# Two message-passing layers on one core: records of four numbers in the first sort, and edge groups in six steps

## The chip, the cores and the metric

The kernel runs on one NeuronCore of a Trainium2 chip. The metric is the time of one execution on the device in microseconds; lower is better. The engines are PE (TensorE: matmuls; PEld are its weight loads), DVE (VectorE), ACT (ScalarE), POOL (GpSimd, which also issues the indirect DMAs, that is gathers and scatters of rows) and SP (SyncE, which here only issues DMAs). Each takes its own instructions in order and waits on semaphores for the others.

## The reference

There are 3125 nodes with 256 features each, and 53125 edges, each with a source, a destination, a type (200 of them) and a weight. `src` comes in any order, `dst` is sorted. Four parts follow one another, each `x = x + part(layernorm(x))`:

```python
# 1: attention over edges, 4 heads of 64
feats = einsum('nd,hdo->hno', x, Ws) + bs
score = a_s[:, src] + a_d[:, dst] + aw_e * elem + ab
w = exp(-relu(score / 20))
out = segment_sum(w * feats[:, dst], src) / segment_sum(w, src)
# 2: 16 experts, the best two per node (silu-gated, hidden 512)
# 3: relations
score = h[src] @ w_src + h[dst] @ w_dst + rel_emb[etype] @ w_rel
alpha = exp(leaky_relu(score)); alpha = alpha / alpha
agg = segment_sum((h[src] + rel_emb[etype]) @ weight_neighbor * alpha, dst)
node = relu(agg) + where(in_degree > 0, h @ loop, h @ evolve_loop)
# 4: the better half of the nodes by a router goes through a 256-1024-256 gelu network
```

## The kernel before

Nodes are held in 25 blocks of 128. A layer over edges needs the edges sorted by the block that they add to.

**Sort of layer 0** (`sort_edges` with `roomy`). The edges lie 416 to a partition. From each edge's three values the kernel makes small whole numbers that float16 holds exactly (`dig`, V of them): the other node, the row in its block plus 1, and the 32 bits of the weight in three pieces of 11, 11 and 10 bits: V is 5. Places are counted with matmuls and scans. Then 13 blocks of columns are moved (`move`): for every eight columns DVE makes one-hot places (L577, L584) and products with the records (L593, one operation for two columns, 40 x V x 2 elements), and PE sums them into PSUM (L598). ACT copies a block's 40 x V numbers out (L606) and POOL scatters them in five indirect DMAs into a table in DRAM (L609). With all 65 scattered, `load` reads the table back (L629), turns it with PE and unpacks it on DVE (L650 to L661, `join_bits`), and writes a wide copy of the rows (`wide`) for later broadcasts. Layer 3's edges are taken in order, without this sort, in pieces that fill the steps of the first edge layer (`fill`).

**Edge layers** (`edge_stages`, `pipelined`). Every block has 18 tiles of 128 edges, the last 8, handled in groups of up to six: 74 groups and 440 tiles in each of the two edge layers. A group goes through three stages, one a step: in step s, group s is gathered, group s-1 becomes messages, group s-2 is added.

- `gather`: six indirect DMAs on POOL fetch the rows (L907) into one of 5 (first layer) or 4 (second) buffers `rows`; DVE makes a one-hot of each edge's row `oh` (L915) and, from the wide copy, transposed ones `hot` (L924).
- `message`: PE picks the near node's numbers with `hot` (L933) into PSUM, DVE sums them (L940), and `messages` makes the weights and scales: in the first layer ACT's exponential (L1097, L1098) and a product of the rows on DVE (L1099); in the second ACT scales `oh` into `ohw` (L1645), and DVE writes a one-hot of the edge type beside the rows (L1639). In a block's second group of the second layer, `loops` (called `early`) transposes the block's features and multiplies them by both loop weights (L200, L202, L1654) into `ps_hold`.
- `add`: PE multiplies `oh` by `rows` into the block's sum (L953, two instructions per tile). After a block's last group DVE reads the sum (L961) and `finish` follows at once. In the first layer it divides and updates x (L1110 to L1113), and at the ends of blocks 5, 10, 15, 20, 23 and 25 the gate's `done` normalizes, transposes and multiplies by the gate's weights (L190, L200, L202, L1196, L1200). In the second layer it turns the type counts (L1666, L1669), multiplies them by the relations (L1672), and DVE reads this and the loop products (L1679 to L1685).

The iota numbers that L915 and L1639 compare with stand in PSUM (`ps_hold`), as do the exponentials that L1099 multiplies by.

**Order.** Tiles, semaphores and the order of instructions on each engine come from a planner that takes the program's order as priority and may move an instruction ahead where its inputs are expected early; `keep_in_program_order` marks an instruction that keeps its place. A tile that is allocated in a full pool waits until the old tile's last reader is done, and the engine that first writes it waits with it.

**After the edges.** `router` prepares the last part, among others by loading its weights w1 and w2 (1 MB each) in a pool that is opened ahead of the second edge layer. `depths` picks the nodes and runs the network (L2016, L2028).

Of the kernel before, what the change touches and what calls it, by code (L numbers as in the profile page):

```python
# [12 lines left out]
I32 = mybir.dt.int32  # L13
AF = mybir.ActivationFunctionType
# [8 lines left out]
class _Kernel:  # L23
# [10 lines left out]


# [261 lines left out]
    def sort_edges(self, pool, rp, name, seg, other, value, bits, tab, help, roomy, into=()):  # L297
# [23 lines left out]
        def load_in():  # L321
# [21 lines left out]
            nc.vector.tensor_scalar(dig[:, 1, :], part, 1.0, None, op0=OP.add)  # L343
            nc.vector.tensor_scalar(dig[:, 0, :], oth_i, -float(self.half), None, op0=OP.add)
            if bits:
                for i, (sh, m) in enumerate(((0, 2047), (11, 2047), (22, 1023))):
                    v = tmp(I32)
                    nc.vector.tensor_scalar(
                        v, vi, sh, m, op0=OP.logical_shift_right, op1=OP.bitwise_and
                    )  # L350
                    nc.scalar.copy(dig[:, 2 + i, :], v)
            else:
                nc.scalar.copy(dig[:, 2, :], vi)
# [264 lines left out]
        def load():  # L618
# [4 lines left out]
            with tc.tile_pool(name=f"{name}_back", bufs=1) as bp:  # L623
# [29 lines left out]
                nc.vector.tensor_scalar(kept(st["row"]), turned(1), -1.0, None, op0=OP.add)  # L653
                for i, w in enumerate(wide):
                    wb = bp.tile([P, nb, P], BF16, name=f"{name}_wb{i}")
                    nc.vector.tensor_copy(wb[:m], tk[:m, :, :, 1 + i])
                    nc.sync.dma_start(w.rearrange("(i k) p -> k i p", k=m), wb[:m])
                if bits:
                    d = [bp.tile([P, MT], I32, name=f"{name}_d{v}") for v in range(3)]
                    for v in range(3):  # L660
                        nc.vector.tensor_copy(kept(d[v]), turned(2 + v))  # L661
                    self.join_bits(st["val"].bitcast(I32), d)
                else:
                    nc.vector.tensor_copy(kept(st["val"]), turned(2))
# [122 lines left out]
    def join_bits(self, out, d):  # L787
        nc = self.nc
        nc.vector.scalar_tensor_tensor(
            d[0], d[1], 11, d[0], op0=OP.logical_shift_left, op1=OP.bitwise_or  # L790
        )
        nc.vector.scalar_tensor_tensor(
            out, d[2], 22, d[0], op0=OP.logical_shift_left, op1=OP.bitwise_or
        )

# [11 lines left out]
    def edges_beyond(self, name, st, table, width, near, W, message, sums):  # L807
# [10 lines left out]
        with tc.If(more > 0):  # L818
            with tc.tile_pool(name=f"{name}_far", bufs=1) as pool:
# [6 lines left out]
                with tc.For_i(0, more) as k:  # L826
# [7 lines left out]
                    nc.vector.tensor_scalar(row, rec[:, 1:2], -1.0, None, op0=OP.add)  # L834
                    if V == 5:
                        d = tl("d", [3], I32)
                        nc.vector.tensor_copy(d, rec[:, 2:5])
                        self.join_bits(val.bitcast(I32), [d[:, i : i + 1] for i in range(3)])
                    else:
# [126 lines left out]
    def pipelined(self, stages, fill=()):  # L966
# [4 lines left out]
        for step in range(len(groups) + len(stages) - 1):  # L971
            if step > 2:
                next(fill, None)
# [1184 lines left out]
```

## Time and profile before

| | |
|---|---|
| median of 6 runs | 2305.77 us (2295.27 to 2313.69) |
| profiled execution | 2309.9 us, span 2308.2 us |
| sort of layer 0 | 0 to 281 us |
| first edge layer | 281 to 988 us |
| experts, and features for the second layer | 988 to 1428 us |
| second edge layer | 1428 to 2168 us |
| choice of nodes and the last network | 2168 to 2308 us |
| busy: PE, DVE, ACT, POOL | 1510.4, 1167.3, 425.5, 1128.8 us |
| mean granted PE clock | 0.799 |

The stages are read from the first and last gathers and from the names of the tiles. A row of the profile names the line, the engine, the operation, the tile written and the tiles read, how often, the busy time and the mean duration of one in ns, and behind the second bar the idle time of the engine just before such instructions with what ended it. "issue" is a wait that the profile can't tie to anything, "remote" a semaphore that was raised at a time where no recorded instruction raises it.

### The profile page before, as it was taken

How to read it: one execution, taken by the hardware profiler on the slowest of the kernel's cores; microseconds unless marked ns; L12 is line 12 of the kernel's file. 1: busy time of each engine (PE TensorE's matmuls, PEld its weight loads, DVE VectorE, ACT ScalarE, POOL GpSimd, SP SyncE). 2: the span in 40 equal slices, each digit the busy share in tenths (PEclk: the TensorE clock that was granted, in tenths of full speed). 3: DMA queues.
4: the chain of work that ended last, by engine and by line, in shares of the span. 5: the costliest groups of instructions: out<-in, count | busy, mean ns of one | idle time of the engine just before them, and what ended most of it. 6: DMA issues, size and time to landing. Idle time of an engine off the chain costs nothing. (4 is left out here: it accounts for less than half of the span.)

```text
span 2308.2 us, 22343 instructions
## 1 busy us (share of the span) xinstructions
PE 1510.4 (65%) x6602; PEld 940.8 (41%) x6602; DVE 1167.3 (51%) x3010; ACT 425.5 (18%) x1148; POOL 1128.8 (49%) x1133
## 2 busy tenths in 40 slices
PE   3688244353533544549999975577777777777588
PEld 1266133342432433426666643233333333333256
DVE  8999435453444643553322234354545555554641
ACT  1311000000101000102122224122222222222421
POOL 1078666656565665413333312455555555565151
PEclk7599667677666776659999988788888888888789
DMA  3050244443444443249999965544444444443230
GB/s 97 25 162 28 67 120 118 129 112 106 127 119 112 114 127 105 73 127 348 302 317 314 316 205 180 151 132 132 132 132 132 132 132 120 132 134 97 74 120 21
DMA packets 250714, 324.52 MB, mean 141 GB/s; under 512 B 38128, under 2 KB 185008, under 8 KB 250582
## 3 DMA queue, kind: packets, MB, share of 16 engines
q1 hardware_dynamic: 192214, 179.00, 25.0%
q0 software_dynamic: 51760, 137.35, 21.1%
q10 hardware_dynamic: 6608, 6.62, 0.8%
q8 instruction: 57, 0.93, 0.2%
q14 instruction: 75, 0.61, 0.1%
HBM read 286.26 MB, written 36.61 MB: 140 GB/s over the span
## 5 line engine op out<-in xcount | busy, mean ns | idle before, releaser
L907 POOL DMA_INDIRECT rows<-table,s_idx x880 | 839.0, 953 | 567.5 <-issue 294.5
L953 PE MATMUL ps_sums<-rows,oh 128*128 128x260 f32 x880 | 271.6, 474 | 246.1 <-issue 244.8
L953 PE MATMUL ps_sums<-rows,ohw 128*128 128x457 f32 x880 | 395.9, 597 | 12.2 <-issue 11.9
L953 PEld LDWEIGHTS ps_sums<-rows,oh 128*128 128x128 f32 x880 | 206.2, 241 | 298.7 <-issue 256.5
L953 PEld LDWEIGHTS ps_sums<-rows,ohw 128*128 128x128 f32 x880 | 177.7, 210 | 185.5 <-issue 171.9
L1387 PE MATMUL ps_h<-w,x_t 128*128 128x512 f32 x448 | 204.6, 599 | 0.0
L915 DVE TENSOR_TENSOR oh<-ps_hold,s_row 128x768 f32<-128x768 f32 (+1 forms) x148 | 139.6, 943 | 124.2 <-remote 74.5
L924 DVE TENSOR_SCALAR hot<-wide,pcols 128x768 bf16<-128x768 bf16 (+1 forms) x296 | 174.4, 596 | 26.5 <-remote 12.5
L1409 POOL DMA_INDIRECT ytab<-y,back x56 | 55.2, 985 | 203.0 <-DVE y L1408 194.2
L1645 ACT ACTIVATE ohw<-oh,s 128x128 f32<-128x128 f32 x440 | 136.8, 392 | 66.5 <-DVE s L1598 26.0
L1654 PE MATMUL ps_hold<-lw,x_t 128*128 128x512 f32 x100 | 78.9, 933 | 106.8 <-DVE oh L915 62.5
L1639 DVE TENSOR_TENSOR rows<-ps_hold,s_val 128x1200 f32<-128x1200 f32 x74 | 103.0, 1392 | 85.8 <-remote 38.1
L940 DVE TENSOR_REDUCE near<-ps_near 128x24 f32<-128x72 f32 (+2 forms) x148 | 29.3, 199 | 228.5 <-remote 200.6
L933 PEld LDWEIGHTS <-hot 128*128 128x128 bf16 x1760 | 64.8, 101 | 183.2 <-DVE hot L924 87.5
L1393 DVE TENSOR_TENSOR hid<-hid,ps_h 128x512 f32<-128x512 f32 x56 | 38.5, 688 | 199.4 <-ACT hid L1392 195.7
L609 POOL DMA_INDIRECT s_tab<-s_rec,s_to x65 | 124.4, 1913 | 30.6 <-issue 19.4
L1099 DVE TENSOR_TENSOR rows<-rows,ps_hold 128x1536 f32<-128x1536 f32 x74 | 128.3, 1734 | 1.0 <-ACT ps_hold L1097 0.3
L1387 PEld LDWEIGHTS ps_h<-w,x_t 128*128 128x128 f32 x448 | 81.8, 193 | 81.1 <-issue 81.0
L1097 ACT ACTIVATE ps_hold<-s 128x24 f32<-128x24 f32 x74 | 14.3, 194 | 504.8 <-DVE s L1093 103.9
L1404 PE MATMUL ps_y<-w,h_t 128*128 128x256 f32 x448 | 105.9, 379 | 0.7 <-ACT h_t L202 0.7
L961 DVE TENSOR_TENSOR acc<-ps_sums,more 128x260 f32<-128x260 f32 (+1 forms) x50 | 26.5, 531 | 157.9 <-remote 94.5
L1362 POOL DMA_INDIRECT xg<-xtab,who x56 | 55.0, 981 | 92.7 <-DVE who_w L1337 62.0
(410 smaller groups left out, 2085.1 us busy)
## 6 DMA issues: line engine op xcount, KB each, us to landing
w<-in_L_ffn_w_dram SPq DMA_DIRECT2D x168, 512.0 KB
wide<-s_w SPq DMA_DIRECT2D x72, 576.0 KB
rows<-table,s_idx POOLq DMA_INDIRECT x880
sums<-sums_z SPq DMA_DIRECT2D x5, 1142.5 KB
more<-sums SPq DMA_DIRECT2D x25, 228.5 KB
yg<-ytab SPq DMA_DIRECT2D x5, 1024.0 KB
sums<-sums_z SPq DMA_DIRECT2D x5, 650.0 KB
table<-f ACTq DMA_DIRECT2D x5, 650.0 KB
```

The costliest lines, as they stand in the source:

```text
L609: d = nc.gpsimd.indirect_dma_start(out=tab, out_offset=bass.IndirectOffsetOnAxis(ap=to[:, i : i + 1], axis=0), in_=out[:, k * CH * V : (k ...
L907: self.last_gather = nc.gpsimd.indirect_dma_start(out=rows[:, j, :width], out_offset=None, in_=table, in_offset=bass.IndirectOffsetOnAxis( ...
L915: nc.vector.tensor_tensor(oh[:, :n, :], numbers[:, None, :P].to_broadcast(sh), st["row"][:, k : k + n, None].to_broadcast(sh), op=OP.is_equal,
L924: nc.vector.tensor_scalar(t[:, : n // 2, :], w, at, None, op0=OP.is_equal)
L933: nc.tensor.matmul(pe[:, j * 3 * nv : (j + 1) * 3 * nv], t[:, j // 2, j % 2 * P : (j % 2 + 1) * P], v.rearrange("p q v -> p (q v)"), start ...
L953: nc.tensor.matmul(ps[:, :W], oh[:, j, :], msg[:, j, :], start=(head and j == 0), stop=(last and j == n - 1),)
L1099: nc.vector.tensor_tensor(rows[:, :n, :HO].rearrange("p j (h o) -> p j h o", o=O), rows[:, :n, :HO].rearrange("p j (h o) -> p j h o", o=O) ...
L1387: nc.tensor.matmul(ph[:, i * HID : (i + 1) * HID], xt[:, c, :], w12[:, i, c, :], start=(c == 0), stop=(c == C - 1),)
L1404: nc.tensor.matmul(py[:, :D], ht[:, c, :], w3[:, c, :], start=(c == 0), stop=(c == HC - 1))
L1639: nc.vector.tensor_tensor(rows[:, :n, R0:], self.numbers[:, None, :R].to_broadcast(sh), st["val"][:, k : k + n, None].to_broadcast(sh), op ...
L1645: nc.scalar.activation(ow[:, j, :], oh[:, j, :], AF.Copy, scale=s[:, 1, j : j + 1])
L1654: nc.tensor.matmul(self.held_ps[:, : 2 * D], ht[:, c, :], lw[:, c].rearrange("p i d -> p (i d)"), start=(c == 0), stop=(c == C - 1),)
```

## The change

The records of the first sort have four numbers: the row and the weight's lowest 4 bits share one (16 x row + bits + 1), and the other 28 bits go in two numbers of 14 bits, written as 16-bit integers plus 1024 whose pattern is taken as float16. `split_row` takes the row and the bits apart again, in `load` for the table and for the wide copy.

An edge group goes through six stages, one a step: gather (with `hot`), pick (the near products and `oh`), message, add, finished (the sum's read, `finish`, and `loops`), closed (in the second layer, the reads of the relations' product and of the loop products). DVE's reads of PE's results are marked to keep their place. The row buffers are 7 and 6. The gate's `done` becomes a generator whose three pieces run in three successive steps, with its logits in `ps_hold`. In the second layer ACT scales `oh` in place, without `ohw`. w1 and w2 are loaded in `depths`, behind the second edge layer.

```diff
             if bits:
-                for i, (sh, m) in enumerate(((0, 2047), (11, 2047), (22, 1023))):
+                low = tmp(I32)
+                nc.vector.tensor_scalar(low, vi, 15, None, op0=OP.bitwise_and)
+                both = tmp(F32)
+                nc.vector.scalar_tensor_tensor(
+                    both, part, 16.0, low, op0=OP.mult, op1=OP.add
+                )
+                nc.scalar.activation(dig[:, 1, :], both, AF.Copy, bias=1.0)
+                for i, sh in enumerate((4, 18)):
                     v = tmp(I32)
                     nc.vector.tensor_scalar(
-                        v, vi, sh, m, op0=OP.logical_shift_right, op1=OP.bitwise_and
-                    )
-                    nc.scalar.copy(dig[:, 2 + i, :], v)
+                        v, vi, sh, 16383, op0=OP.logical_shift_right, op1=OP.bitwise_and
+                    )
+                    nc.vector.tensor_scalar(
+                        dig[:, 2 + i, :].bitcast(I16), v, float(self.LEAST), None, op0=OP.add
+                    )
...
+                    self.split_row(
+                        bp.tile([P, nb, P], I32, name=f"{name}_wl")[:m],
+                        bp.tile([P, nb, P], I32, name=f"{name}_wh")[:m], tk[:m, :, :, 1],
+                        wb := bp.tile([P, nb, P], BF16, name=f"{name}_wb")[:m], 1.0,
+                    )
...
+                    self.split_row(kept(d[0]), kept(d[1]), turned(1), kept(st["row"]), 0.0)
+                    for v in (1, 2):
+                        nc.vector.tensor_scalar(
+                            kept(d[v]), turned(1 + v).bitcast(I16), float(self.LEAST), 0.0,
+                            op0=OP.subtract, op1=OP.max,
+                        )
...
+    def split_row(self, low, high, src, row, add):
+        nc = self.nc
+        nc.vector.tensor_scalar(low, src, -1.0, None, op0=OP.add)
+        nc.vector.tensor_scalar(high, low, 4, None, op0=OP.arith_shift_right)
+        nc.vector.tensor_scalar(row, high, add, None, op0=OP.add)
+        nc.vector.tensor_scalar(low, low, 15, None, op0=OP.bitwise_and)
...
-        def message(g, b, k, n, head, last, rows, oh, hots):
-            pe = self.ps_b("ps_near")
+        def pick(z, b, k, n, head, last):
+            z["pe"] = pe = self.ps_b("ps_near")
...
+            z["oh"] = oh = pool.tile([P, G, P], F32, name="oh", bufs=4)
...
+        def message(z, b, k, n, head, last):
             own = pool.tile([P, G, nv], F32, name="near")
-            nc.vector.tensor_reduce(
+            self.tc.keep_in_program_order(nc.vector.tensor_reduce(
...
+            messages(k, n, z["rows"], own, z["oh"])
+
+        def add(z, b, k, n, head, last):
...
+        def finished(z, b, k, n, head, last):
             if early is not None and k - self.first[b] == G:
                 early(b)
...
             if last:
                 acc = pool.tile([P, W], F32, name="acc")
-                nc.vector.tensor_add(acc, ps[:, :W], more)
-                finish(b, acc)
-
-        return gather, message, add
+                self.tc.keep_in_program_order(
+                    nc.vector.tensor_add(acc, z["sum"][:, :W], z["more"])
+                )
+                z["done"] = finish(b, acc)
+
+        def closed(z, b, k, n, head, last):
+            if last and close is not None:
+                close(b, z["done"])
+
+        return gather, pick, message, add, finished, closed
...
+            for p in pending:
+                next(p, None)
...
-                pool, st, self.table0, W, W, near, [], messages, W, self.sums0, finish, deep=5
-            ), fill)
+                pool, st, self.table0, W, W, near, [], messages, W, self.sums0, finish, deep=7
+            ), fill, pending)
...
-            pl = self.ps_b("ps_logit")
+            yield
+            pl = self.held_ps[:, 256:512]
...
-                ow = pool.tile([P, G, P], F32, name="ohw", bufs=3)
                 for j in range(n):
                     nc.scalar.activation(
-                        ow[:, j, :], oh[:, j, :], AF.Copy, scale=s[:, 1, j : j + 1]
-                    )
-                return ow, rows
+                        oh[:, j, :], oh[:, j, :], AF.Copy, scale=s[:, 1, j : j + 1]
+                    )
...
-                early=loops, deep=4,
+                close=close, early=loops, deep=6,
...
-        tab0, tab1 = self.edge_table("s0", 5), self.edge_table("s1", 3)
+        tab0, tab1 = self.edge_table("s0", 4), self.edge_table("s1", 3)
```

## The prediction

> **What bounds the kernel now.** I read the windows first, to split the span by stage: sort moves and their scatters, first edge layer, second edge layer.
>
> ```profile
> 107.00:268.00 161.00, 111.32 (x616) 83.46 (x616) 138.69 (x321) 23.25 (x64) 127.56 (x67) 0.86 0.27 82
> 281.00:988.00 707.00, 318.70 (x1468) 250.68 (x1468) 341.98 (x829) 56.71 (x191) 422.94 (x445) 0.69 0.42 114
> 1428.00:2168.00 740.00, 542.24 (x2500) 268.70 (x2501) 381.81 (x1009) 187.82 (x615) 416.41 (x439) 0.84 0.47 133
> ```
>
> Columns: stretch, length, busy PE, PEld, DVE, ACT, POOL, granted clock, DMA share, GB/s. The edge layers are 1447 of 2308 us, and in neither is an engine full. Each is 74 groups of mostly six gathers, 440 gathers. The rows of the gather line, one window per layer, give the pace:
>
> ```profile
> L907 POOL DMA_INDIRECT rows<-table,s_idx x440: 943/949/1307, 281.2 to 958.5; - x147
> ```
>
> ```profile
> L907 POOL DMA_INDIRECT rows<-table,s_idx x440: 943/949/1085, 1426.5 to 2144.0; - x147
> ```
>
> One gather lasts 0.95 us and follows the last after 0.30, so an unhindered pace is 1.254 us (the median step between starts in the timeline), 7.52 us for a group. 439 steps of 1.254 are 550.5 us. The first layer takes 677.3 (958.5 - 281.2), the second 717.6: POOL is held for 126.8 and 167.1 us. That is all the edge part can give while the gathers stay on POOL. The timeline of POOL shows what a hold looks like, and the waits say who is late:
>
> ```profile
> 1932.97 0.95 POOL L907 DMA_INDIRECT rows<-table,s_idx  x1 [0.30 <-issue]
> 1934.23 0.95 POOL L907 DMA_INDIRECT rows<-table,s_idx  x1 [0.30 <-issue]
> 1942.61 0.95 POOL L907 DMA_INDIRECT rows<-table,s_idx  x1 [7.43 <-PE ps_sums L953]
> ```
>
> ```profile
> ACT x_t L202 <- remote: 222.7, 32, 11.2
> DVE near L940 <- remote: 200.6, 34, 19.9
> ...
> POOL rows L907 <- PE ps_sums L953: 186.1, 36, 16.8
> ...
> DVE acc L961 <- remote: 94.5, 14, 14.2
> ```
>
> POOL waits for a row buffer, which frees when PE has added the group. DVE stands in L940 and L961 for results that PE was given in the same step; everything behind them in DVE's queue (L924, L915, the multiply L1099) waits too, and PE's next add waits for that. "remote" is a semaphore the trace ties to no instruction; here it is one that PE raises, 6 us late on average (200.6/34). In the first layer the holds are one per block of three groups, some 3 to 4.5 us, and 14.4, 13.2, 13.5 and 16.5 at the four gates (steps between group starts less 7.52). In the second they come in pairs of blocks: 58.1 us for six groups against 45.1.
>
> In the sort, DVE and POOL move in step; the groups by line, then POOL's timeline:
>
> ```profile
> L593 DVE TENSOR_TENSOR s_hv<-s_hk,s_dig 128x400 f16<-128x400 f16 x208 | 92.3, 515 | 0.0
> ...
> L584 DVE TENSOR_TENSOR s_hk<-num_k,s_kp 128x320 f16<-128x320 f16 x52 | 23.1, 447 | 0.0
> ```
>
> ```profile
> 239.71 2.25 POOL L609 DMA_INDIRECT s_tab<-s_rec,s_to  x1 [0.30 <-issue]
> 242.27 2.28 POOL L609 DMA_INDIRECT s_tab<-s_rec,s_to  x1 [0.30 <-issue]
> 244.85 0.96 POOL L609 DMA_INDIRECT s_tab<-s_rec,s_to  x1 [0.30 <-issue]
> 246.11 0.96 POOL L609 DMA_INDIRECT s_tab<-s_rec,s_to  x1 [0.30 <-issue]
> ```
>
> A set of eight columns costs DVE 2.64 us, and one scatter goes out per set, 2.63 apart. When DVE stops at 247 the remaining 18 scatters run 1.265 apart until 267, and only then is the table read back.
>
> **Part 1, records of four numbers.** L593 works on 320 elements, not 400, 208 times. L584 does 320 elements in 447 ns where L593 takes 515: 0.068 x 208 = 14 us; in proportion to the elements it would be 20% of 92.3 = 18.5. I take 16. The scatters keep one to a set of columns, as the rows show, so their end moves by the same 16. If they kept 2.63 whatever DVE does, 6 of them (16/2.63) would move behind DVE's end at 1.265 and only 8 would be won. Against that: the digits at the start become six DVE operations on 416 elements instead of four (about +1 us, DVE is full there). Reading back, the table's fields need 13 operations of 0.4 to 0.6 us instead of 8, about +2 us straight ahead of the first gather. Sum -13, bounds -5 and -15. The smaller zero fill, scatter packets, 160-wide matmuls and 64-byte records lie beside DVE and POOL: nothing.
>
> A scatter lasts 2.3 us beside L584 and L593, which read SBUF twice; a gather stays at 0.95 beside L915, L1099 and L1639, which read one side from PSUM (ps_hold), and the sum goes by that row. The Trainium skill's page GPSIMD Engine Reference, section Key points, says that POOL shares its SBUF interfaces with VectorE and contends with instructions of two SBUF inputs. By that rule a busier DVE (L924 has one input, the small L1093 and L1094 two) could stretch single gathers to the scatters' 2.3.
>
> **Part 2, six steps.** Nothing per group is added or removed: 12 adds, the near products, L940, L915 and the message are the same instructions; the tile ohw goes, ACT scales oh in place, with a fourth buffer. What moves: near products one step ahead of L940; the sum's read (L961) a step behind the last add; the gate in three pieces over three steps; in the second layer ps_rel is read (L1679) a step after its matmuls. Row buffers go from 5 to 7 and from 4 to 6, while a buffer is held one step longer, so POOL may run one group, 7.5 us, further ahead.
>
> Is there room for 7.52 us a group? First layer: DVE 341.98/74 = 4.6 us, PE 318.70/74 = 4.3, both at the present clock. Second: DVE 381.81/74 = 5.2, PE 542.24/74 = 7.3 at a clock of 0.84, 6.2 if it were full. So the first layer can reach POOL's pace, the second barely.
>
> First layer: the holds at plain block ends (126.8 less 57.6 of the gates = 69) go, since L961 waits for an add that is a step old; I leave 8. The gates keep the chain of transposes on PE, copies on ACT (L202, remote) and products inside one step; their 57.6 us lose 7.5 each to the deeper buffers: 28 left. Gain 127 - 36 = 91. Bounds: 127 won, or nothing; below nothing is the last rival.
>
> Second layer: L940 and L961 come off the chain, but the loop products keep their transposes, copy and L1654 in one step, 7 us of PE standing still per pair of blocks. 44 us of PE work for six groups plus half of the stall on top gives about 50 where POOL wants 45: 74/6 x 5 = 62, and some 15 for single late results. Gain 167 - 77 = 90. Bounds: 167, or 25% of it (42).
>
> Matmuls L953 start 0.38 us apart at the granted clock of 1.0 and 0.86 after a standstill, at 0.5 (the rows near 1675 and 1680 us). The Trainium skill's page TensorE: Matmul & The Clock Gate, section What's actually happening, says that an idle window of about 3.4 us halves the clock. Even steps leave PE idle for less than that; by the rule PE in the second layer would need 6.2 of the 7.52 us and another 30 us could go.
>
> Behind the last gather 29.7 and 24.5 us of work are left; three more steps each cost at most a step of DVE (5 us) and mostly overlap: +2 each, bounds 0 and +15. What waits behind the new DVE reads is the next hot and oh of DVE, and through them PE.
>
> **Part 3, w1 and w2** (2 MB) load when the edge layer's buffers are free, about its end at 2168, where they used to load at its beginning. First use is L2016 at 2209. At the 120 GB/s of these slices 2 MB takes 17 us: hidden by the 41 us of choosing rows. On SP's queue they may stand ahead of the ztab writes (19 us, done at 2174, needed by the gathers after 2200): still hidden; with no cover it would cost up to 17. I take 0.
>
> **Sum.** The profiled execution took 2309.9 us (span 2308.2), 4 above the median of 2305.8. 2309.9 - 13 - 91 - 90 + 4 = 2120; less the 4, **2116 us**. Its own range is 2050 to 2180: 62 and 15 more or less of the layers' remains, and the sort's bounds.
>
> **Rivals.** *PE is the chain.* If the late semaphores mean that PE truly works that long, the second layer gains only its 25% (42) and the first its gates' buffers and half of the plain holds (30 + 35): -13 - 42 - 65 + 4 = -116, 2190 us. For it: PE's 7.3 us per group. Against it: in the first layer PE is busy 45%.
>
> *It changes no order.* DVE's rows show L924 of later groups ahead of L940 already, so the instructions' order, which a planner makes, may be much the same; then the sort's -13 alone remains: 2293. Against it: the rows of L961 do stand waiting.
>
> *A pinned read holds DVE (slower).* L940, L961 and L1679 now keep their place in DVE's queue. Where PE is later than a step, DVE cannot pass them, and L924, L915 and the messages of all following groups stand behind. At the 5.9 us of a remote wait plus 2 us until PE is warm again, once per block: 25 x 8 = 200 us of holds per layer instead of 127 and 167: +73 + 33 - 13 + 4 = +97, 2403 us. It decides from the point where a group takes longer than the present 9.28 (677.3/73) and 9.83 us (717.6/73).
>
> **How the numbers follow.** Forecast 0.58, PE as the chain 0.20, no new order 0.05, pinned reads 0.17. Faster by over 0.5% is the first two: 0.78. Within 0.5% (about what a measurement of this kernel can tell from no change) 0.05, slower 0.17. The range takes in the first three cases, 2050 to 2310, and leaves out the last and a little below.
>
> **What would show it.** L593 at 320 elements near 1.45 us for four, the first gather near 268; the gathers' first-to-last at about 587 and 628 us; "POOL rows <- PE ps_sums" well under 100 us; the waits of L940 and L961 nearly gone, those of x_t on ACT still there; a granted clock over 0.84 in the second layer. Wrong: gather pace unchanged with the same holds, gathers longer than 1 us, or PE idle ahead of L2016 for longer than now.

## The result, and the profile after

The changed kernel takes 2326.92 us (median of 20 runs, 2318.42 to 2333.44) where the kernel before takes 2304.51 us (46 runs on the same chip): ratio 1.0099, interval 1.0080 to 1.0117. It is 1% slower. The forecast was 2116 us, the range ended at 2310. The profiled execution took 2326.8 us with a span of 2324.4.

The stages, read from the first and the last start in the rows of the gathers:

| | before | after | change | forecast |
|---|---|---|---|---|
| to the first gather | 281.2 | 267.2 | -14.0 | -13 |
| first layer, first to last gather | 677.3 | 655.5 | -21.8 | -91 |
| last gather to the second layer's first | 468.0 | 473.4 | +5.4 | +2 |
| second layer, first to last gather | 717.6 | 745.6 | +28.0 | -90 |
| last gather to the end | 164.2 | 182.7 | +18.5 | +2 |
| span | 2308.2 | 2324.4 | +16.2 | -190 |

The rows of the gather line, one window for each layer (count, then shortest/median/longest in ns, then first and last start):

```profile
L948 POOL DMA_INDIRECT rows<-table,s_idx x440: 940/946/1503, 267.2 to 922.8; - x147
L948 POOL DMA_INDIRECT rows<-table,s_idx x440: 940/946/991, 1396.1 to 2141.7; - x147
```

A gather is as long as it was and follows the last after the same 0.30 us; only the holds between gathers differ. In the windows by stage (busy PE, PEld, DVE, ACT, POOL, granted clock, DMA share, GB/s) no engine is full, and the clock in the second layer fell from 0.84 to 0.81 instead of rising:

```profile
267.00:950.00 683.00, 329.82 (x1464) 259.81 (x1464) 349.76 (x798) 53.56 (x187) 420.39 (x440) 0.70 0.43 118
1396.00:2168.00 772.00, 502.49 (x2463) 260.58 (x2464) 386.92 (x1003) 178.55 (x606) 415.96 (x440) 0.81 0.45 125
```

The list of waits (sum in us, times, longest) says who stands now:

```profile
PEld ps_cnt L1722 <- DVE acc L1008: 231.7, 25, 11.7
DVE hot L959 <- remote: 215.4, 27, 23.8
...
DVE hot L959 <- PE ps_sums L994: 158.9, 35, 8.2
...
POOL rows L948 <- PE ps_sums L994: 80.5, 21, 18.7
...
POOL rows L948 <- DVE x L1745: 65.1, 10, 6.8
...
POOL rows L948 <- remote: 56.6, 21, 3.6
ACT x_t L206 <- remote: 55.1, 6, 18.8
```

The near numbers' remote wait (200.6 us at L940) is gone from the top of the list, that of the transposes (x_t, 222.7) fell to 55.1. In their place DVE waits as long at L959, the first instruction of a new group: it needs the buffer of a `hot` tile, which PE's near products of two groups earlier must have released. And PE stands at the type counts (L1722), whose input L1008 has to wait behind it on DVE. The waits moved; they did not go.

What such a wait is, in the timelines of PE, DVE and POOL (start, length, and the idle time before with its releaser):

```profile
399.81 0.30 PE L967 MATMUL ps_near<-near0p,hot 128*128 128x12 bf16 x6
```

```profile
413.48 0.61 DVE L959 TENSOR_SCALAR hot<-wide,pcols 128x768 bf16<-128x768 bf16 x1 [13.37 <-remote]
```

```profile
409.31 0.95 POOL L948 DMA_INDIRECT rows<-table,s_idx  x1 [0.30 <-issue]
414.11 0.94 POOL L948 DMA_INDIRECT rows<-table,s_idx  x1 [3.86 <-issue]
```

PE finished the near products at 400.1, and DVE, which waits for PE's semaphore alone, started at 413.48: PE's signal took 13.4 us. (The ends of matmuls in the profile are modelled, so it can't tell a late signal from a late end; "late signal" below stands for both.) POOL meanwhile issued gathers until 410.3, when its row buffers were used up. Only then did the signal that DVE waited for come, 3.2 us after the last gather, and the hold ended with it.

### The profile page after: what moved, and what is told of

Read it like the earlier page. It is cut to its first block, busy times and chain, and to the rows that moved or that the text cites. A ratio compares the mean times of both kernels' runs of the same rounds, so it can differ in the third digit from the quotient of the medians.

```text
span 2324.4 us, 22247 instructions
## 1 busy us (share of the span) xinstructions
PE 1484.9 (64%) x6598; PEld 941.5 (41%) x6598; DVE 1177.0 (51%) x3017; ACT 414.9 (18%) x1146; POOL 1112.3 (48%) x1133
## 5 line engine op out<-in xcount | busy, mean ns | idle before, releaser
L994 PE MATMUL ps_sums<-rows,oh 128*128 128x260 f32 (+1 forms) x1760 | 698.9, 553 | 268.8 <-issue 267.7
L994 PEld LDWEIGHTS ps_sums<-rows,oh 128*128 128x128 f32 x1760 | 394.4, 233 | 480.0 <-issue 419.3
L959 DVE TENSOR_SCALAR hot<-wide,pcols 128x768 bf16<-128x768 bf16 (+1 forms) x296 | 173.5, 601 | 484.5 <-remote 215.4
L975 DVE TENSOR_TENSOR oh<-ps_hold,s_row 128x768 f32<-128x768 f32 (+1 forms) x148 | 139.7, 944 | 82.5 <-remote 58.8
L1722 PE MATMUL ps_cnt<-ident,acc 128*128 128x128 f32 (+1 forms) x50 | 20.1, 401 | 217.7 <-DVE acc L1008 150.9
L1702 ACT ACTIVATE oh<-oh,s 128x128 f32<-128x128 f32 x440 | 137.8, 390 | 62.7 <-DVE s L1656 34.1
L624 POOL DMA_INDIRECT s_tab<-s_rec,s_to x65 | 111.6, 1717 | 29.4 <-issue 19.1
L967 PEld LDWEIGHTS <-hot 128*128 128x128 bf16 x1760 | 70.6, 99 | 115.7 <-issue 63.3
L1722 PEld LDWEIGHTS ps_cnt<-ident,acc 128*128 128x128 f32 (+1 forms) x50 | 7.7, 153 | 242.6 <-DVE acc L1008 231.7
L1462 PEld LDWEIGHTS ps_y<-w,h_t 128*128 128x128 f32 x448 | 85.0, 190 | 36.0 <-issue 26.3
L1654 ACT ACTIVATE s<-s 128x6 f32<-128x6 f32 x74 | 15.3, 207 | 443.9 <-DVE s L1653 398.2
L608 DVE TENSOR_TENSOR s_hv<-s_hk,s_dig 128x320 f16<-128x320 f16 x208 | 83.0, 559 | 0.0
```

Source lines behind the costliest of these rows:

```text
L608: nc.vector.tensor_tensor(rec[:, i], hk[:, i, :, None, :].to_broadcast(sh), dig[:, None, :, t0 + 2 * i : t0 + 2 * i + 2].to_broadcast(sh), ...
L624: d = nc.gpsimd.indirect_dma_start(out=tab, out_offset=bass.IndirectOffsetOnAxis(ap=to[:, i : i + 1], axis=0), in_=out[:, k * CH * V : (k ...
L959: nc.vector.tensor_scalar(t[:, : n // 2, :], w, at, None, op0=OP.is_equal)
L967: nc.tensor.matmul(pe[:, j * 3 * nv : (j + 1) * 3 * nv], t[:, j // 2, j % 2 * P : (j % 2 + 1) * P], v.rearrange("p q v -> p (q v)"), start ...
L975: nc.vector.tensor_tensor(oh[:, :n, :], numbers[:, None, :P].to_broadcast(sh), st["row"][:, k : k + n, None].to_broadcast(sh), op=OP.is_equal,
L994: nc.tensor.matmul(ps[:, :W], z["oh"][:, j, :], z["rows"][:, j, :], start=(head and j == 0), stop=(last and j == n - 1),)
```

## The experiments

The runs fell on different chips, each with its own runs of the kernel before; ratios are to those. The chips are called B to F (the first comparison was on A; whether A is one of the others is not on record). Layers 0 and 1 are the first and the second edge layer. Stages from the gather rows of each profile, in us. They are of one execution each, which can lie some 10 us from its kernel's median (e4: 2316.1 against 2326.4), and the kernel before differs by 1.7% among A to E, so a difference of 10 us between two chips' stages says little:

| kernel (chip, before there) | median | ratio, interval | first gather | layer 0 | between | layer 1 | behind |
|---|---|---|---|---|---|---|---|
| after (A, 2304.5) | 2326.9 | 1.0099, 1.0080 to 1.0117 | 267.2 | 655.5 | 473.4 | 745.6 | 182.7 |
| e1_sort (B, 2298.7) | 2273.0 | 0.9877, 0.9823 to 0.9931 | 267.0 | 676.0 | 465.7 | 698.6 | 164.2 |
| e2_nomarks (B) | 2346.0 | 1.0182, 1.0125 to 1.0238 | 267.9 | 663.3 | 473.6 | 770.0 | 177.8 |
| e3_oldest (B) | 2286.6 | 0.9927, 0.9893 to 0.9962 | 267.7 | 654.4 | 473.6 | 707.2 | 181.8 |
| e6_sumread (B) | 2316.6 | 1.0061, 1.0033 to 1.0089 | 266.4 | 640.9 | 474.1 | 750.9 | 183.3 |
| e4_hot3 (C, 2333.4) | 2326.4 | 0.9967, 0.9936 to 0.9999 | 267.3 | 654.3 | 470.9 | 743.2 | 178.8 |
| e5_oldest_hot3 (C) | 2286.0 | 0.9794, 0.9754 to 0.9834 | 267.7 | 653.3 | 474.1 | 724.3 | 172.6 |
| e7_near1 (C) | 2304.0 | 0.9891, 0.9862 to 0.9920 | 265.3 | 654.1 | 533.4 | 665.0 | 185.0 |
| e8_halfgather (C) | 1938.8 | 0.8323, 0.8296 to 0.8350 | 265.5 | 437.1 | 537.3 | 513.6 | 186.1 |
| e9_before_half (D, 2293.4) | 1891.1 | 0.8238, 0.8211 to 0.8265 | 282.4 | 409.4 | 530.1 | 503.1 | 166.4 |
| e10_onehot (D) | 2325.1 | 1.0121, 1.0095 to 1.0147 | 267.5 | 656.0 | 476.9 | 746.6 | 182.2 |
| e11_nodep (D) | 2308.5 | 1.0052, 1.0024 to 1.0080 | 266.2 | 646.0 | 476.9 | 725.9 | 181.7 |
| e12_both (D) | 2301.6 | 1.0042, 1.0013 to 1.0070 | 264.6 | 646.2 | 477.1 | 723.0 | 182.5 |
| e13_narrow (E, 2327.2) | 2431.4 | 1.0451, 1.0431 to 1.0472 | 266.9 | 661.9 | 533.7 | 783.7 | 182.9 |
| e14_pace (E) | 2413.8 | 1.0376, 1.0339 to 1.0412 | 266.3 | 691.8 | 470.9 | 791.2 | 185.0 |
| e15_oldest_both (E) | 2292.9 | 0.9865, 0.9845 to 0.9885 | 264.1 | 651.4 | 473.3 | 710.3 | 185.0 |
| e16_sort_nodep (E) | 2303.5 | 0.9916, 0.9888 to 0.9944 | 265.7 | 683.8 | 464.7 | 715.3 | 167.5 |
| e18_oldest_hot3_nodep (F, 2010.1) | 2008.9 | 0.9995, 0.9985 to 1.0004 | 266.9 | 553.9 | 466.8 | 550.0 | 168.4 |
| e19_sort_again (F) | 1996.7 | 0.9934, 0.9918 to 0.9951 | 267.8 | 554.9 | 453.2 | 554.8 | 165.8 |

### The sort alone

**e1_sort** is the kernel before with the new sort alone: edge layers, gate and the loading of w1 and w2 are as before.

> The sort with records of four numbers alone; edge layers, gate and the loading of w1 and w2 as before. If the parts simply add up, the first gather comes at about 267 us (281.2 before, 267.2 after) and the whole is 13 to 14 us shorter than before, about 2291 us. If the shorter sort is given back behind it (the pieces of the other sort that fill the first edge layer, or experts that wait for their weights), the time stays within 5 us of 2305.

It is 1.2% faster, 25.7 us, some 12 more than expected. 14 us are the sort (first gather at 267.0); the second layer, whose program is the same, came out 19 us shorter than in the profile of before, on another chip, and why is not shown. So it is the rest of the change and not the sort that made the kernel slower: against e1 the changed kernel is 20 us shorter in the first layer, 8 longer between the layers, 47 longer in the second, 18 longer behind the last gather.

### Marks, order, place of the sum's read

**e2_nomarks**: the four `keep_in_program_order` of the edge layers are taken off.

> The changed kernel with the four marks gone that pin the reads of PE's results (near numbers, block sum, gate, relations); the steps are the same. If the pins make DVE read the block sum so late that PE stands at the transposes of the counts (231.7 us in 25 waits in the changed kernel), this wait falls under 100 us, the second layer's gathers go from 745.6 us to 700 or less, and the time to about 2280 us. If the place of the read in the program and not the mark does it, the wait and the time stay (2320 to 2330 us).

**e3_oldest**: a step's stages are written from the oldest group to the newest.

```diff
-            for i, stage in enumerate(stages):
+            for i, stage in reversed(list(enumerate(stages))):
```

> The changed kernel with the six parts of a step written in the opposite order, the oldest group's first: close, sum read, adds, messages, near products, gather. DVE then has the sum read ahead of the two younger groups' operations. If PE's wait for the sum read is what slows the second layer, PE's wait at the count transposes falls from 231.7 to under 80 us, the second layer's gathers from 745.6 to about 680 us, and the time to about 2260 us. If the late semaphores behind the near products set the pace, DVE waits at the hots instead (215 us in the changed kernel, then over 300), and the time stays at 2310 to 2330 us.

**e6_sumread**: L1008 and `finish` go back to the step of the last add and are not marked.

```diff
                 nc.sync.dma_start(more, sums[b])
+                acc = pool.tile([P, W], F32, name="acc")
+                nc.vector.tensor_add(acc, z["sum"][:, :W], z["more"])
+                z["done"] = finish(b, acc)
```

> The changed kernel with the read of the block sum and what follows it at once (finish) back in the step of the last add, unpinned, as before the change; near products, gate and the relations' read stay in their new steps. If the read held a group behind costs the second layer its time, PE's wait at the count transposes falls to about the 40 us of before, the second layer's gathers to 718 us or less, the work behind the last gather by about 5 us, and the time to about 2290 us. If not, 2320 to 2330 us.

Without the marks it is slower (the second layer 770.0), so the pinned reads are not what costs. Putting the sum's read back helps the first layer by 15 us and not the second (750.9). The order of the stages matters most: with the oldest group first the second layer takes 707.2, 38 us less, though not the 680 hoped for. PE's wait at the counts nearly goes in both (231.7 us in the changed kernel; e3, then e6):

```profile
PEld ps_cnt L1722 <- DVE acc L1008: 25.0, 23, 7.7
```

```profile
PEld ps_cnt L1719 <- DVE acc L1002: 36.6, 25, 1.5
```

Since e6's second layer is no shorter for it, that wait by itself is not what the second layer lost. And the late results are still there in e3, at other places:

```profile
DVE near L982 <- remote: 155.6, 17, 26.1
...
ACT ct L1725 <- PE ps_cnt L1722: 146.8, 25, 7.6
...
DVE hot L959 <- remote: 104.6, 16, 13.7
```

### More buffers, less work on PE, half the gathers

**e4_hot3**: three buffers of each `hot` tile, and 5 row buffers instead of 6 in the second layer to make room. **e5_oldest_hot3**: the same with e3's order.

> The changed kernel with three buffers for the transposed one-hots instead of two; to make room the second layer has 5 row buffers instead of 6. If DVE stands at the hots because a hot buffer comes free only with the late semaphore of the near products two groups back (215.4 us remote and 158.9 us behind ps_sums in the changed kernel), this wait falls under 100 us; a block of the second layer, 30.7 us in the changed kernel, comes to about 27 us and the time to about 2240 us. If PE itself is that late, the wait only moves on (to the read of the near numbers or the sum) and the time stays at 2310 to 2330 us.

> The same three buffers and 5 row buffers, with the parts of a step written oldest group first. If the hots' buffers and the place of the sum read both held the pace, the two add up: about 2200 us. If PE's late semaphores set the pace by themselves, it comes to the 2287 us of the opposite order alone, within 10.

Buffers alone leave both layers as long as they were on A (654.3 and 743.2). By its ratio e4 is 1.3% better off than the changed kernel, though it takes as long (2326.4 and 2326.9 us), since the kernel before is slowest on C. The changed kernel was not run there, so a gain of the buffers on C is neither shown nor ruled out. e4 and e5, on one chip, differ in the order alone: 2326.4 against 2286.0 us, 40 us for the order. e5 has the best ratio on a late chip, 0.9794, though its second layer is not shorter than e3's.

**e7_near1**: one near product for a group's six tiles and each `hot` tile, instead of one for each tile. The near numbers are wrong, so other experts are chosen.

> The changed kernel with one near product for each pick of a group instead of one for each tile (1 instead of 6 in the first layer, 3 instead of 18 in the second): the near numbers of the first tile stand for all six. All other work stays. If the many small near products with their weight loads are what raises PE's semaphores late (6.6 us in the second layer), the lag falls under 1 us, POOL goes without holds (7.5 us a group) and each layer's gathers come to 560 to 600 us: about 2120 us in all. If the lag comes from something else that goes on at that time, it stays at 4 to 7 us, and the time at about 2300 us.

**e8_halfgather**: every second gather becomes a plain load of 128 fixed rows from SP. **e9_before_half** is the same in the kernel before.

```diff
             for j in range(n):
+                if j % 2:
+                    nc.sync.dma_start(rows[:, j, :width], table[b * P : (b + 1) * P, :])
+                    continue
```

> The changed kernel with every second gather of an edge layer replaced by a plain load of 128 rows in a row, issued by SP; the sums are of other rows, the bytes and all products the same. POOL then needs 3.8 us for a group instead of 7.5. If PE's late semaphores come with POOL's gathers, the lag falls and a group comes down to about the 5 to 6 us of DVE and PE: the time falls by over 300 us. If the chain of PE, DVE and ACT is as slow without them, a block of the second layer stays at about 30 us and the first layer's at 26, and the time within 50 us of 2327.

> Leaves out every second gather: 128 rows of a fixed place are loaded plainly in its stead, so the numbers differ and 65 expert tiles are expected instead of 56 (about +64 us in the experts, as in e8). It is the partner of e8 for the steps of before. Theory A (TensorE's semaphores come late only while GpSimd issues gathers back to back, and the six steps lose by that alone): with half the gathers both are prompt, and before's steps are then slower than those of after by what the prediction took for the pinned reads and the held results, at least 40 us in layer 1 beside e8's 513.6 us; in all 1970 to 2030 against e8's 1939. Theory B (the six steps cost TensorE or VectorE work of their own): before's steps are as fast or faster with half gathers too, layer 1 490 to 515 us, in all 1905 to 1955 (with the sort's 13 us).

All three run the experts for 65 tiles instead of 56 (PE's rows of ps_h count 520 instead of 448), some 64 us in the column "between". e7 takes the second layer from 745.6 to 665.0 and leaves the first at 654.1. Between that layer's gathers "remote" waits still sum to 173.6 us (179.9 in the changed kernel), so the signals stay late while less work on PE gives 80 us: on a late chip PE's work in the second layer counts as well. With half the gathers (e8) the late signals shrink. Counted from the recorded end of an instruction that raises PE's semaphore to the next update that the trace holds, 163 of 714 in the changed kernel's second layer are over 3 us late, and 10 of 706 in e8's. But PE is then the bound, with before's steps too:

```profile
1300.00:1750.00 450.00, 410.31 (x2158) 213.89 (x2158) 327.31 (x819) 140.86 (x501) 178.59 (x189) 0.98 0.61 176
```

410 of 450 us at a clock of 0.98 is e8; e9 has 452 of 490. The six steps are not shorter here: 437 against 409 in the first layer, 514 against 503 in the second (on two chips). So theory A's 40 us of gain did not appear; e9's second layer is where theory B has it, and its time is below both ranges.

### Is it the number of signals, the bytes, or the pace?

The first theory was a backlog: TensorE's signals pass slowly while GpSimd gathers, and the changed kernel has more of them (714 recorded instructions that raise its semaphore between the second layer's first and last gather, against 545). **e10_onehot** makes the three `hot` tiles of a group one tile, **e11_nodep** takes the gathers' own signals off the adds (the message's DVE work has waited for the rows), **e12_both** does both.

```diff
+                self.tc.add_to_no_dep_group(f"rows{W}_{k}", self.last_gather.ins)
...
+                self.tc.declare_no_dep(
+                    m.ins, group=f"rows{W}_{k}", reason="the message's sum waits for all rows"
+                )
```

> The three hot tiles of a group become one tile, so that they come free by one signal of TensorE and not by three. By the program, TensorE's instructions that raise its semaphore fall in layer 1 from 726 to 582 and in layer 0 by a third of a near product each. Theory A (the raises trickle while GpSimd gathers, and come at some 1.77 in a us in its holds): 144 fewer at 1.77 in a us are 81 us less in layer 1, 745.6 to 650..700, in all 2230 to 2270, ratio to before 0.965 to 0.985. Theory B (the lateness doesn't depend on the number of raises): 2315 to 2340, ratio 1.005 to 1.015.

> The adds of a pick no longer wait on the gathers' own signals (the message's VectorE work, which they wait for, has waited for all the rows). By the program TensorE's raises fall in layer 0 from 502 to 148 and in layer 1 from 726 to 583. Theory A: layer 0's holds (108 us after) mostly go, 655.5 to 560..600 us; layer 1 745.6 to 650..700; in all 2130 to 2210, ratio 0.92 to 0.96. Theory B: 2315 to 2340, ratio 1.005 to 1.015.

> Both edits, one hot tile and adds without the gathers' signals: raises 148 in layer 0, 439 in layer 1. Theory A: layer 0 560 to 600 us, layer 1 560 to 640 us, in all 2040 to 2150, ratio 0.89 to 0.935. Theory B: 2315 to 2340, ratio 1.005 to 1.015. If only e10 or only e11 gains, raises of one kind matter and their number alone does not.

The theory falls. A fifth fewer signals (e10) change nothing; 70% fewer in the first layer (e11, e12) give 10 us of a hoped-for 60 to 90, and there 94 of e12's 165 raises still come over 1 us late (220 of 493 in the changed kernel). Dropping the adds' waits is worth 24 us in all (e10 against e12, on one chip: 2325.1 and 2301.6), most of it in the second layer, and that is all.

**e13_narrow** keeps the issue of all gathers and takes most of their bytes (32 of a row's 257 or 260 numbers; a plain load for each group brings the rest from fixed rows). **e14_pace** puts a memset between gathers.

```diff
+                nc.gpsimd.memset(pool.tile([P, P], F32, name="pace", bufs=1), 0.0)
```

> GpSimd issues the same 880 gathers, but each fetches 32 of a row's 257 or 260 numbers (and from a place that is not the row's own); one plain load for a group brings the other columns from fixed rows. So the numbers differ, and 65 expert tiles (+64 us) are likely as in e8. Theory A (TensorE's raises are held while the gathers' packets move): with an eighth of the bytes the packets leave gaps, the raises pass as in e8, layer 0 560 to 610 us, layer 1 580 to 670 us, in all 2090 to 2230. Theory B (GpSimd's issuing back to back holds them, or the holds are the steps' own): layer 0 640 to 665, layer 1 720 to 755, in all 2310 to 2400.

> A memset of 128x128 on GpSimd (204 ns in the profile) behind every gather, so that gathers come every 1.46 us or more instead of 1.25, and their packets leave gaps; 439 steps of 1.46 are 641 us for a layer. Theory A (gaps between the packets let TensorE's raises pass, so the long holds shrink): layer 0 645 to 690, layer 1 660 to 720, in all 2230 to 2320. Theory B (the holds are not changed by the pace): the 88 us of a layer's memsets come on top where GpSimd sets the end; layer 0 720 to 750, layer 1 770 to 835, in all 2420 to 2500.

e13's first layer is where theory B put it, its second layer and the whole are beyond. With an eighth of the gathered bytes DVE still waits at the same place, longer than in the changed kernel (the list of waits of e13):

```profile
DVE hot L964 <- remote: 403.4, 42, 18.6
```

So it is not the bytes that gathers move. The bytes in all stayed, since the plain loads bring the rest; e8 kept them too, with fewer late signals. e14 tests little: its 880 memsets stand in 204 places between gathers, 138 of them alone and the others in rows of several, and a single one fills most of the 0.30 us that lies between gathers anyway, which then come every 1.34 us instead of 1.25:

```profile
300.76 0.95 POOL L948 DMA_INDIRECT rows<-table,s_idx  x1 [0.17 <-issue]
301.71 0.23 POOL L954 MEMSET pace<- 128x128 f32 x1
302.09 0.95 POOL L948 DMA_INDIRECT rows<-table,s_idx  x1 [0.16 <-issue]
```

The layers became 36 and 46 us longer; more than that can't be read from it. What these two have in common with the changed kernel is that GpSimd issues 880 gathers, and so has e7.

### The best forms, and a chip without late signals

**e15_oldest_both** is e12 in e3's order, **e16_sort_nodep** is e1 with e11's edit, **e18_oldest_hot3_nodep** is e5 with e11's edit, **e19_sort_again** is e1 unchanged.

> The six steps with the oldest group's stage written first (e3), one hot tile and adds without the gathers' own signals (e12). If the gains add: e3's 38 us in layer 1 and e12's 10 and 22 us make 2255 to 2265, ratio 0.97 to 0.985. If both ease the same hold: 2275 to 2290, ratio 0.988 to 0.996.

> Before's steps with the new sort (e1) and the adds without the gathers' own signals. If that wait costs before's steps as it cost the six (30 us in two layers): 2235 to 2250, ratio 0.968 to 0.98, and it is the fastest of all. If the six steps alone suffer from it: as e1, 2265 to 2280, ratio 0.983 to 0.993.

> The six steps with the oldest group's stage written first, a third buffer of the hot tiles (and five row buffers in layer 1 to make room), and the adds without the gathers' own signals. If a VectorE that never waits for TensorE's old near products is what is still missing: ratio 0.965 to 0.98, below e19 by 1% or more. If the three ease one and the same hold: ratio 0.98 to 0.99, within 0.6% of e19.

> The sort's four numbers alone, steps of before (e1 once more, beside e18 on one chip): ratio 0.982 to 0.994, the sort's 14 us of 2305 (0.6%) and at most as much again in layer 1.

None of the gains add: e15 lies between its two cases, e18 in neither of its own, and e16 is no better than e1 by its ratio (0.9916, 0.9877), so the adds' waits cost before's steps nothing that shows. Are the six steps in their best order ahead of before's steps with the same sort? On chip E yes, 0.9865 against 0.9916 (e15, e16). On chip B no, 0.9927 against 0.9877 (e3, e1), with intervals that overlap. On chip F they are behind, 0.9995 against 0.9934. But the larger fact is the time itself: on F the kernel before takes 2010 us, not 2300. e1 and e19 are one and the same program, 2273.0 us on B and 1996.7 on F. The gather rows of e1, then of e19:

```profile
L945 POOL DMA_INDIRECT rows<-table,s_idx x440: 940/946/1499, 267.0 to 943.0; - x147
L945 POOL DMA_INDIRECT rows<-table,s_idx x440: 940/946/1136, 1408.7 to 2107.2; - x147
```

```profile
L945 POOL DMA_INDIRECT rows<-table,s_idx x440: 942/947/1494, 267.8 to 822.7; - x147
L945 POOL DMA_INDIRECT rows<-table,s_idx x440: 942/947/1162, 1275.8 to 1830.6; - x147
```

On F both layers run at the gathers' own pace (554.9 and 554.8 us against 439 x 1.254 = 550.5). Of the 275 us between the spans, 121 lie in the first layer, 144 in the second and 12 between them. In the waits of e1 stand

```profile
ACT x_t L206 <- remote: 176.9, 24, 14.3
...
POOL rows L945 <- PE ps_sums L991: 163.3, 34, 16.5
...
DVE near L978 <- remote: 146.4, 30, 10.8
...
DVE acc L999 <- remote: 111.3, 11, 15.5
```

and among the 197 longest of e19 there is no "remote" at all. Over 3 us late, as counted above, are 96 of 545 raises in e1's second layer and none of 551 in e19's. POOL's wait for a row buffer in e19:

```profile
POOL rows L945 <- PE ps_sums L991: 13.4, 30, 4.7
```

One pair of rows shows the difference, PE's transposes and ACT's copy that waits for them. In e1 the transposes end at 1720.00 and the copy starts 6.26 us later; in e19 they end at 1522.99 and it starts after 0.03:

```profile
1719.59 0.41 PE L204 MATMUL ps_x_t<-ident,xn 128*128 128x128 f32 x2
```

```profile
1726.26 0.37 ACT L206 COPY x_t<-ps_x_t 128x256 f32<-128x256 f32 x1 [7.72 <-remote]
```

```profile
1522.57 0.42 PE L204 MATMUL ps_x_t<-ident,xn 128*128 128x128 f32 x2
```

```profile
1523.02 0.37 ACT L206 COPY x_t<-ps_x_t 128x256 f32<-128x256 f32 x1 [1.50 <-PE ps_x_t L204]
```

With signals in time there is nothing for six steps to win: e18's layers take 553.9 and 550.0. What is left of them is their price. e18's span is 9.5 us longer than e19's, and the largest part, 13.6, lies between the layers: the experts' first gather starts 58.8 us behind the last row gather in e18 (879.6 - 820.8) and 47.1 in e19 (869.8 - 822.7), where the last groups and the gate's last pieces go through more steps:

```profile
L1424 POOL DMA_INDIRECT xg<-xtab,who x56: 946/963/1699, 879.6 to 1186.5; - x56
```

```profile
L1400 POOL DMA_INDIRECT xg<-xtab,who x56: 942/965/1117, 869.8 to 1177.1; - x56
```

The changed kernel itself was not run on F; e18 is the nearest form.

## Why the prediction was wrong

**Sort, -13: right.** The first gather came 14.0 us earlier, and on F the whole gain of e19, which differs from before in the sort alone, is 13.4 us. The path was as told, the rows were not: L608 on 320 elements is not shorter one by one (559 ns against 515) nor is L599 on the same 320 (572 against 447), yet a set of eight columns takes 2.35 us instead of 2.63 (median distance of scatters). Neighbours overlap on DVE in this profile, and their durations can't be multiplied; the distance from scatter to scatter could:

```profile
204.04 2.13 POOL L624 DMA_INDIRECT s_tab<-s_rec,s_to  x1 [0.30 <-issue]
206.48 1.98 POOL L624 DMA_INDIRECT s_tab<-s_rec,s_to  x1 [0.30 <-issue]
208.76 1.99 POOL L624 DMA_INDIRECT s_tab<-s_rec,s_to  x1 [0.30 <-issue]
```

**Gathers beside DVE: right.** They took 946 ns, 949 before. The Trainium skill's GPSIMD Engine Reference, section Key points, has POOL contend with VectorE's instructions of two SBUF inputs. The rows agree for the scatters (2 us and more beside L608), and the gathers show no such stretch.

**First layer, -91: the gates right, the plain holds wrong.** The steps over the four gates are now 14.4, 17.4, 16.1 and 16.9 us between group starts, 34.7 above pace where 28 was forecast (57.6 before). The plain block ends were to fall from 69 to 8 and stayed at 105 - 35 = 70. ("POOL rows <- PE ps_sums" fell under 100 us, as the prediction's sign had it, and yet the holds stayed: POOL's waits went to other releasers.)

**Second layer, -90: wrong in sign.** A block of three groups takes some 7.5 + 10 + 13.5 = 31 us, where 29 was normal before.

**The step that failed** is one sentence that both layers used: DVE's late reads "go, since L961 waits for an add that is a step old". It takes a late signal for a delay of fixed length, 6 us, which a step of 7.5 us covers. On the chips where it is late, TensorE's signal has no such length. It is 13.4 us in the rows shown and anything from 0 to 17 behind the near products of other groups; the prediction's 6 us (200.6/34) was DVE's mean idle time and not the signal's delay. Most signals come when GpSimd stops: the semaphore's updates that the trace holds (574 for the 714 raises in the changed kernel's second layer) come at 0.38 in a us while GpSimd gathers and at some 1.8 in its holds. A hold ends with such an update, so this alone doesn't say which of the two causes the other. My reading is that GpSimd stops when its row buffers are used up, so a step more distance or two buffers more move the hold and do not end it. The layers of e4 agree for the `hot` buffers, and the wait that left L940 stands at L959.

**Why slower, not merely the same.** The order written newest first costs some 40 us (e4 against e5 on one chip; 38 in e3's second layer), the adds' waits for the gathers' signals some 24 (e10 against e12). e3, e5 and e15, which are without the first, are the six-step forms with all their gathers and products that clearly beat the kernel before on these chips, by about what the new sort alone gives (e1, e16). That the order decides is shown. How it does so is not: that DVE stands at L959 ahead of older groups' reads, with PE behind it at the counts, was the reading of the waits, and in e6 PE's wait at the counts is nearly gone (36.6 us) and the second layer no shorter.

**Behind the last gather, +2: 18.5.** That is above the upper bound of 15. With six steps the last groups drain through late signals as well; on F, in e18, the same drain costs 2.6 (168.4 - 165.8), and the first layer's 11.7 (58.8 - 47.1).

**w1 and w2, 0: right.** PE does not wait longer ahead of L2076 than it did ahead of L2016; from the network's first matmul to the end it takes 100.2 us instead of 99.0.

**The rivals.** "PE is the chain" is out as the whole cause: with signals in time PE has room (e19 on F, the second layer at the gathers' pace, granted clock 0.94), and its forecast, 2190 us, was missed too. But e7 shows that on a late chip PE's work in the second layer is worth up to 80 us. "A pinned read holds DVE" had the sign and not the mechanism: without the marks it is slower still (e2), and DVE is held by an unmarked instruction. "It changes no order" is out by e3 and e6. By the clock rule of the Trainium skill's page TensorE: Matmul & The Clock Gate, section What's actually happening, the prediction estimated another 30 us if the steps became even. They did not, and the clock fell to 0.81; on F, where the gathers run at their pace, it is 0.94.

**What the page of before showed and I passed over.** 679 us of "remote" waits, a semaphore raised where no instruction ends, were read as one engine's delay of fixed length. The Trainium skill's page Perfetto Trace Analysis, section Tensor Engine Instruction (MATMUL, LD_WEIGHTS), has the signal leave after PSUM's acknowledgement, outside the window that the profiler reports; it gives no time for it. The runs here have both: 0.03 us in the pair of rows from F, 6.26 in that from B.

## What to carry to other kernels

A wait whose releaser ends long before it is not a dependency that one can plan around: before restructuring for it, find out whether the lateness has a fixed length, and run the unchanged kernel on a second chip. Price an overlapped stretch by the distance between the instructions that leave it, not by the mean of the rows inside. And in a software pipeline, write the oldest group's stage first where a queue may stand: here the order alone was worth 40 us of 2300, and six stages in the better order were not clearly ahead of three.

## What was not expected of the hardware

The same program takes 2273.0 us on one chip and 1996.7 on another, with the same durations of gathers (946 and 947 ns). What the traces show different is TensorE's signals. On chips A to E (before 2293 to 2333 us) they are late in the edge layers, up to 17 us, while GpSimd issues gathers one behind the other, and prompt in the experts' stage (none of 213 raises over 1 us late in the changed kernel), where its 56 gathers come some 5.6 us apart. On F (before 2010) neither of the two profiles has such a wait. What differs in chip F, and whether it is the issue of gathers that delays the signals or something that goes with it, these runs don't show: fewer signals (e10, e12) and fewer gathered bytes (e13) did not cure it, and with half as many gathers (e8) the delays were shorter. The slower pace (e14) was too little to tell.

Of the versions run, the four-number sort with before's steps beat the kernel before on both kinds of chip (0.9877 and 0.9934). The six steps in the oldest-first order, with the same sort, beat it by up to 2.1% on a late chip (e5, on C, where the sort alone was not run) and by nothing on F (e18).
